# A scan layer and a convolution-attention layer: POOL's C product in two instructions, and inputs of the second layer put elsewhere

## The chip, the cores and the metric

The kernel runs on one core of a Trainium2 chip. A core has five engines that run side by side, each through its own instructions in order: PE (TensorE, matrix products), DVE (VectorE), ACT (ScalarE), POOL (GpSimd) and SP (SyncE, which here only issues transfers). ACT issues transfers too. Engines wait for each other at semaphores. The metric is the device time of the program in microseconds; of several runs the median is taken.

## The reference

Four images of 512 channels and 32 x 32 pixels go through two layers, each with a residual sum and a group normalisation in front. All is float32.

```python
x = x + L0(_gn(x), ...)
# L0, per image, L = 1024 tokens, 1024 inner channels, 16 states:
xn = layernorm(x over channels) * ln_w + ln_b
xm, z = split(xn @ W_in)
xs = silu(causal_depthwise_conv4(xm) + conv_b)
proj = xs @ W_x                      # 32 for dt, 16 for B, 16 for C
dt = softplus(proj[..., :32] @ W_dt + b_dt)
def step(h, inp):
    dt_t, B_t, C_t, x_t = inp
    h = exp(dt_t[..., None] * A) * h + (dt_t * x_t)[..., None] * B_t[:, None, :]
    return (h, einsum('bds,bs->bd', h, C_t))
y = scan(step) + xs * D
out = (y * silu(z)) @ W_out

x = x + L1(_gn(x), ...)
# L1, per image:
top, center = conv1x1(x, w_top), conv1x1(x, w_center)      # 64 channels each
bottom = conv3x3(x, w_bottom)
sp = softmax over all (n, m) of center^T top
x2 = x + (sp @ bottom) reshaped as it lies in memory
out = conv3x3(x2, w_out)
```

## The kernel before

**First layer.** The work is cut into units: image b, a pair of channel chunks e (2 x 128 channels), a half of the tokens h (512), and a state s: 4 x 4 x 2 x 16 = 512 units. A unit is written in `unit` (from line 814). ACT forms the decay exp(dt A) for each of the two chunks (L832). The input dt x B comes in one of two ways. For the nine states in `B_ON_ACT`, ACT scales rows (L844) and PE turns them into PSUM (L870). For the other seven, POOL multiplies (L859) with a broadcast row of B that SP fetches. DVE runs the recurrence as two scans, one for each chunk (L884), and in the first half copies the last column to a carry (L889). Then comes the product with C: for the four states in `C_ON_DVE` on DVE, per chunk (L900); for the other twelve on POOL, in one instruction over both chunks, 128 x 1024 elements (L906). PE adds the product of each chunk into its accumulator y (L913), turned back to tokens.

The order of the instructions is not that of the program text. Each piece of work is handed to `step` with its engine, a cost in us, what it reads and writes, and a priority; `Plan.issue` (from line 104) then plays the five engines forward with these costs and emits each instruction when its engine would take it. Buffers come in rings of a few slots: four for `h` (the tiles named da), four for `dbx`, five for `cbc` (broadcast rows of C). A slot is free again when its last user is done. The four `parts` and the tile `hc` tell the planner which chunk's scan a product needs: the product on POOL writes both parts, so it is placed after both scans, and both additions after it. Marked as filling, `transform` places on POOL the 18 pieces of weight transforms of the 3 x 3 convolutions; they go where there is room.

**Second layer.** The 3 x 3 convolutions are done with transformed tiles of the image and weights (6 row places in pairs (1, 2), (3, 4), (0, 5), 4 column places): `conv3` (L1439). Each of its 24 places is four accumulating matmuls of 128 x 512 (L1494), with a weight of 1 MB that SP loads into a ring of three (L1490). ACT and DVE evacuate the sums (L1502, L1510), and POOL adds them up (L1515, L1523, L1524, L1531). The inputs of a pair come from `first_inputs` (ACT L1393, POOL L1394, DVE L1396 and L1397) or `inputs`, then four DVE instructions in `spread` (L1374 to L1377).

For each pair of images a and a + 1 the order of the text is: conv3 b of image a, `attend(a)`, `scores(a + 1)`, conv3 b of a + 1, `attend(a + 1)`, conv3 o of a and `finish(a)`, conv3 o of a + 1 and `finish(a + 1)`, `scores(a + 2)`. In traces and text b0, o0, b1, o1 are these convolutions by image. `scores` makes eight tiles of scores, tag `st`, ring of eight: PE (L1324, then L1345), ACT copies them from PSUM (L1349), DVE takes maxima (L1350), ACT the exponentials (L1359). `attend` multiplies them with the convolution (L1546), in eight groups, and DVE adds each to the image (L1559). In the first two attentions it also does pieces of the output weights on DVE (L1421 to L1432). The PSUM ring `ps` of three serves scores, attention, statistics and `finish`; `pm` of five serves conv3.

`norm(b)` makes the next image: it takes the zero-bordered tile (`padded`, POOL memsets), loads the first layer's result in eight transfers on ACT's queue (L1285) into a tile with the tag `v`, which is that of the convolution's inputs (ring of two), and takes statistics on DVE (L1292, L1293). Two small PE products over the groups (L1299, L1303) and two ACT steps follow, then DVE normalises (L1306). Image 1's and image 3's norm runs beside the attention before; image 2's runs as `mid` inside conv3 o1. Images 0 and 2 share one buffer, 1 and 3 another.

In this layer the framework orders the instructions of an engine by its own estimate of readiness, within the dependencies. So a later function's instruction can stand ahead of an earlier one's on the same engine.

Of the kernel before, what the change touches and what calls it, by code (L numbers as in the profile page):

```python
# [8 lines left out]
F32 = mybir.dt.float32  # L9
# [6 lines left out]
P = 128  # L16
B, C, HH, WW = 4, 512, 32, 32
L = HH * WW
NCC = C // P
# [4 lines left out]
T = 512  # L24
# [145 lines left out]
def mamba_then_pab_kernel(  # L170
# [25 lines left out]
    nc = tc.nc  # L196
# [23 lines left out]
    brow = []  # L220
# [53 lines left out]
    with ExitStack() as l0:  # L274
# [539 lines left out]
        def unit(b, e, h, s, y):  # L814
# [86 lines left out]
                        [u, c_bc], [part], prio, holds=[hc],  # L901
                    )
            if not on_dve:
                step(
                    "POOL", 2.31,
                    lambda: nc.gpsimd.tensor_mul(hc(), hc(), c_bc().to_broadcast([P, 2, T])),  # L906
                    [c_bc], parts, prio, holds=[hc],
                )
            for j in range(2):

                def add(j=j):
# [348 lines left out]
    with ExitStack() as l1:  # L1260
# [15 lines left out]
        NMC = L // P  # L1276
        HR = T // WW

        def norm(b):

            xg = padded(b, *((cpool, "image"), (gp, "xg"))[b % 2])
            t = xp.tile([P, NCC, L], F32, tag="v", name=f"x1t_{b}")
            for c in range(NCC):
                for h in range(NH):
                    nc.scalar.dma_start(  # L1285
                        t[:, c, h * T : (h + 1) * T], x1[b][h][c * P : (c + 1) * P, :]
                    )
            mv = spool.tile([P, NCC, 2], F32, tag="mv", name=f"mv_l1_{b}")
            for c in range(NCC):
                bs = spool.tile([P, NH, 6], F32, tag="bs", name=f"bs_l1_{b}_{c}")  # L1290
                for h in range(NH):
                    nc.vector.bn_stats(bs[:, h, :], t[:, c, h * T : (h + 1) * T])  # L1292
                nc.vector.bn_aggr(mv[:, c, :], bs)  # L1293
            mean, rstd, dev = (
                spool.tile([P, NCC], F32, tag=n, name=f"{n}_l1_{b}")
                for n in ("gmean", "grstd", "gdev")
            )
            p1 = ps.tile([P, T], F32, tag="ps", name=f"pm_l1_{b}")
            nc.tensor.matmul(p1[:, :NCC], gm_sb, mv[:, :, 0], start=True, stop=True)  # L1299
            deviation(p1, mv, mean, dev)  # L1300
            yield
            p2 = ps.tile([P, T], F32, tag="ps", name=f"pv_l1_{b}")
            nc.tensor.matmul(p2[:, :NCC], gm_sb, dev, start=True, stop=True)  # L1303
            rsqrt(rstd, p2[:, :NCC])
            for c in range(NCC):
                nc.vector.tensor_scalar(  # L1306
                    xg[:, c, 1 : HH + 1, 1 : WW + 1],
                    t[:, c].rearrange("p (h w) -> p h w", w=WW),
                    mean[:, c : c + 1], rstd[:, c : c + 1], ALU.subtract, ALU.mult,
                )  # L1310
            image[b] = xg

        def scores(b, xg):

# [121 lines left out]
            for q in (1, 2):  # L1436
                nc.sync.dma_start(dst[q], o[:, q - 1])

        def conv3(name, xg, u, bias, first=None, late=None, mid=None):  # L1439

# [34 lines left out]
            y = [None] * 4  # L1475
            for pair in PAIRS:
                if pair == (1, 2):
                    v = first or first_inputs(name, xg)
                    if mid:
                        mid()  # L1480
                else:
                    v = spread(name, pair[0], inputs(pair))
                ns = []
                for k, p in enumerate(pair):
                    m = {}
                    for q in (2, 1, 0, 3):
                        if late and (p, q) == (5, 3):
                            late(y)
                        w = fp.tile([P, NCC, C], F32, tag="u", name=f"uw_{name}_{p}_{q}", bufs=3)
                        nc.sync.dma_start(w, u[q][p])  # L1490
                        m[q] = pm.tile([P, C], F32, tag="m", name=f"m_{name}_{p}_{q}")
                        extra = (p, q) == (1, 1)
                        for c in range(NCC):
                            nc.tensor.matmul(  # L1494
                                m[q], v[:, q, k, c, :], w[:, c, :],
                                start=(c == 0), stop=(c == NCC - 1 and not extra),
                            )
                        if extra:
                            nc.tensor.matmul(m[q], ones[0:1, :], bias, start=False, stop=True)
                    al = ALPHA[p]  # L1500
                    e = lp.tile([P, C], F32, tag="e2", name=f"e2_{name}_{p}", bufs=2)
                    nc.scalar.activation(e, m[2], AF.Copy, scale=al / 2)  # L1502
                    n = lp.tile([P, 2, C], F32, tag="n", name=f"n_{name}_{p}", bufs=2)
                    for o, src, w, add, op in (
                        (n[:, 0], m[1], al / 2, e, ALU.add),
                        (n[:, 1], m[1], al / 2, e, ALU.subtract),
                        (n[:, 0], m[0], al, n[:, 0], ALU.add),
                        (n[:, 1], m[3], -al, n[:, 1], ALU.add),
                    ):
# [25 lines left out]
            return y  # L1535

        def attend(b, xg, st, rp, xb, between, also):
# [4 lines left out]
            for k in range(NCC * NH):  # L1542
# [8 lines left out]
                if k == 0:  # L1551
# [4 lines left out]
                    for _ in between:  # L1556
                        pass
                img = xg[:, j, 1 + h * HR : 1 + (h + 1) * HR, 1 : WW + 1]
                nc.vector.scalar_tensor_tensor(  # L1559
                    img, pt.rearrange("p (h w) -> p h w", w=WW), rz, img,  # L1560
                    ALU.mult, ALU.add,
                )
                if also:
                    taps = piece_taps(also[k + 1]) if k + 1 < len(also) else None
                    piece(*ahead)
                    ahead = taps
                    if taps is None:
                        also = []

        dst = [out[b].rearrange("(c p) h w -> p c (h w)", p=P) for b in range(B)]  # L1570

# [41 lines left out]
                turn_back(b, j, o[j], y, 1)  # L1613
                (nc.scalar, nc.sync)[j % 2].dma_start(dst[b][:, j, :], o[j])

        def normed(b):
            for _ in norm(b):
                pass

        left = list(range(EARLY, NPC))  # L1620
        half = len(left) // 2
        st, rp = scores(0, image[0])
        for a in range(0, B, 2):
            for b in (a, a + 1):
                xb = conv3(f"b{b}", image[b], ub, brow[0])
                also = left[b * half : (b + 1) * half] if not a else []
                after, v = iter(()), None
                if b == a:
                    after = norm(b + 1)
                    next(after)  # L1630
                else:
                    v = first_inputs(f"o{a}", image[a])
                attend(b, image[b], st, rp, xb, after, also)
                if b == a:
                    st, rp = scores(b + 1, image[b + 1])
            finish(a, conv3(f"o{a}", image[a], uo, brow[1], v))
            if a + 2 == B:
                last(a + 1, image[a + 1], None)
                break
            y = conv3(f"o{a + 1}", image[a + 1], uo, brow[1], mid=lambda: normed(a + 2))  # L1640
            finish(a + 1, y)
            st, rp = scores(a + 2, image[a + 2])


# [55 lines left out]
```

## Time and profile before

| what | us |
|---|---|
| median of 3 runs | 3060.0 (3053.99 to 3060.22) |
| the profiled execution | 3048.93 |
| its span | 3047.1 |
| DVE busy in the span | 2402.3 |
| PE busy in the span | 2742.4 |
| POOL busy in the span | 2022.1 |
| ACT busy in the span | 1842.4 |

A profile line of a group gives source line, engine, operation, output and inputs by tile name, sizes and count, then after a bar the total busy us, the mean ns of one, and the engine's idle time just before the group with what ended most of it. A timeline line gives start and length in us, engine, line, what was done and how often; in square brackets how long the engine stood idle before and who released it. PE's records of a float32 product come in pairs: four matmuls show as x8. The share of a busy PE is not its share of peak.

### The profile page before, as it was taken

How to read it: one execution, taken by the hardware profiler on the slowest of the kernel's cores; microseconds unless marked ns; L12 is line 12 of the kernel's file. 1: busy time of each engine (PE TensorE's matmuls, PEld its weight loads, DVE VectorE, ACT ScalarE, POOL GpSimd, SP SyncE). 2: the span in 40 equal slices, each digit the busy share in tenths (PEclk: the TensorE clock that was granted, in tenths of full speed). 3: DMA queues.
4: the chain of work that ended last, by engine and by line, in shares of the span. 5: the costliest groups of instructions: out<-in, count | busy, mean ns of one | idle time of the engine just before them, and what ended most of it. 6: DMA issues, size and time to landing. Idle time of an engine off the chain costs nothing.

```text
span 3047.1 us, 35912 instructions
## 1 busy us (share of the span) xinstructions
PE 2742.4 (90%) x11512; PEld 1607.5 (53%) x11512; DVE 2402.3 (79%) x3171; ACT 1842.4 (60%) x3179; POOL 2022.1 (66%) x1047
## 2 busy tenths in 40 slices
PE   4789789999889999889999978799899999999998
PEld 2346556656666666556666655544344444444444
DVE  3469999989999989989999999976857575456164
ACT  4579989998789999789999888731110013030000
POOL 7899977899967889967889999843321331323132
PEclk8899999999999999989999999999999999999999
DMA  6766534567734567734566654748588896727497
GB/s 179 213 192 210 168 121 141 164 207 231 232 109 145 166 180 229 251 116 133 168 184 213 209 177 141 171 154 297 170 286 263 301 330 246 264 70 275 138 316 256
DMA packets 408947, 610.47 MB, mean 200 GB/s; under 512 B 46488, under 2 KB 245400, under 8 KB 384184
## 3 DMA queue, kind: packets, MB, share of 16 engines
q1 hardware_dynamic: 399952, 593.67, 61.8%
q10 hardware_dynamic: 8648, 14.26, 1.3%
q8 instruction: 92, 1.51, 0.2%
q14 instruction: 95, 0.78, 0.1%
q0 software_dynamic: 160, 0.26, 0.0%
HBM read 511.09 MB, written 96.99 MB: 200 GB/s over the span
## 4 chain that ended last, share of the span: by engine, by line
PE 45%; DVE 23%; ACT 16%; DMA 6%; issue 5%; POOL 4%; SPq 1%; ACTq 0%; DVEq 0%; POOLq 0%
PE m_o L1494 10%; PE m_b L1494 9%; DVE da L884 7%; PE y L913 5%; PE pz L394 4%; ACT sc L844 4%; PE pat L1546 4%; DVE u L884 3%; ACT da L832 3%; PE po L394 2%; PE u L870 2%; ACT u L832 2%; DVE dbx L884 2%; PE pxm L394 2%; PE psc L1345 2%
## 5 line engine op out<-in xcount | busy, mean ns | idle before, releaser
L906 POOL TENSOR_TENSOR da<-da,cbc 128x1024 f32<-128x1024 f32 x288 | 680.3, 2367 | 151.3 <-DVE carry_sb L889 63.6
L859 POOL TENSOR_TENSOR dbx<-dtx,bbc 128x1024 f32<-128x1024 f32 x224 | 529.6, 2368 | 59.1 <-PE y L913 34.9
L844 ACT ACTIVATE sc<-dtxt,bt_sb 128x256 f32<-128x256 f32 x1152 | 504.6, 497 | 46.2 <-PE u L870 46.0
L832 ACT ACTIVATE da<-dt,a_sb 128x512 f32<-128x512 f32 x576 | 395.0, 713 | 39.2 <-PE y L913 33.5
L884 DVE TENSOR_TENSOR_SCAN da<-da,carry_sb,u 128x512 f32<-128x512 f32 x288 | 356.0, 1262 | 27.3 <-PE u L870 22.0
L913 PE MATMUL y<-ident,da 128*128 128x128 f32 x2304 | 320.4, 283 | 58.3 <-POOL da L906 54.4
L870 PE MATMUL u<-ident,sc 128*128 128x128 f32 x2304 | 336.1, 278 | 35.3 <-DVE da L884 24.9
L913 PEld LDWEIGHTS y<-ident,da 128*128 128x128 f32 x2304 | 268.5, 145 | 161.2 <-POOL da L906 109.9
L884 DVE TENSOR_TENSOR_SCAN da<-da,u 128x512 f32<-128x512 f32 x288 | 348.8, 1211 | 3.9 <-PE u L870 3.6
L1494 PE MATMUL m_o<-uw_o,v_o 128*128 128x512 f32 x768 | 337.9, 599 | 4.4 <-DMA uw_o<-u_o 4.4
L1494 PE MATMUL m_b<-uw_b,v_b 128*128 128x512 f32 x768 | 333.4, 593 | 4.1 <-DMA uw_b<-u_b 4.1
L870 PEld LDWEIGHTS u<-ident,sc 128*128 128x128 f32 x2304 | 268.4, 143 | 112.2 <-DVE da L884 37.2
L832 ACT ACTIVATE u<-dt,a_sb 128x512 f32<-128x512 f32 x448 | 297.4, 681 | 36.8 <-DVE dbx L900 14.0
L394 PE MATMUL pxm<-xt,winc 128*128 128x345 f32 (+3 forms) x704 | 251.3, 499 | 29.3 <-DMA winc<-in_w_in_dram 16.5
L913 PE MATMUL y<-ident,dbx 128*128 128x128 f32 x1792 | 252.9, 279 | 23.7 <-POOL dbx L906 14.4
L913 PEld LDWEIGHTS y<-ident,dbx 128*128 128x128 f32 x1792 | 207.5, 143 | 99.7 <-issue 32.2
L394 PE MATMUL pz<-xt,winc 128*128 128x512 f32 x512 | 242.1, 600 | 11.7 <-ACT sz L707 2.1
L1494 PEld LDWEIGHTS m_o<-uw_o,v_o 128*128 128x128 f32 x768 | 145.9, 192 | 188.0 <-issue 180.7
L1494 PEld LDWEIGHTS m_b<-uw_b,v_b 128*128 128x128 f32 x768 | 145.0, 190 | 188.9 <-issue 179.5
L906 POOL TENSOR_TENSOR dbx<-dbx,cbc 128x1024 f32<-128x1024 f32 x96 | 226.7, 2362 | 26.0 <-DVE carry_sb L889 17.5
L1546 PE MATMUL pat<-y_b,st 128*128 128x512 f32 x512 | 221.6, 593 | 1.6 <-DVE rz L1555 1.5
L394 PEld LDWEIGHTS pxm<-xt,winc 128*128 128x128 f32 x704 | 132.0, 198 | 117.1 <-issue 62.1
(235 smaller groups left out, 4331.5 us busy)
## 6 DMA issues: line engine op xcount, KB each, us to landing
cbc<-bcd SPq DMA_DIRECT2D x512, 256.0 KB, 3.6
uw_b<-u_b SPq DMA_DIRECT2D x96, 1024.0 KB, 4.8
uw_o<-u_o SPq DMA_DIRECT2D x96, 1024.0 KB, 4.8
bbc<-bcd SPq DMA_DIRECT2D x224, 256.0 KB, 3.6
u_b<-work SPq DMA_DIRECT2D x192, 128.0 KB, 2.8
winc<-in_w_in_dram SPq DMA_DIRECT2D x72, 256.0 KB, 3.8
szd<-sz SPq DMA_DIRECT2D x32, 512.0 KB, 3.5
szl<-szd SPq DMA_DIRECT2D x32, 512.0 KB, 5.0
```

The costliest lines, as they stand in the source:

```text
L394: lambda k=k, lhs=lhs, rhs=rhs: nc.tensor.matmul(p()[:, at : at + cols], lhs(), rhs(), start=(k == 0), stop=(k == n - 1)),
L832: nc.scalar.activation(t, dt()[:, j], AF.Exp, scale=a_sb[:, at : at + 1])
L844: nc.scalar.activation(sc()[:, k], dtxt()[:, k], AF.Copy, scale=bt[:, at, s : s + 1])
L859: lambda: nc.gpsimd.tensor_mul(hc(), dtx(), b_bc().to_broadcast([P, 2, T])),
L870: nc.tensor.transpose(u()[:, k * P : (k + 1) * P], sc()[:, k, j, :], ident)
L884: nc.vector.tensor_tensor_scan(ht, *((hc()[:, j], u()) if on_act else (u(), hc()[:, j])), carry_sb[:, j, s : s + 1] if h else 0.0, ALU.mul ...
L906: lambda: nc.gpsimd.tensor_mul(hc(), hc(), c_bc().to_broadcast([P, 2, T])),
L913: nc.tensor.matmul(y[j]()[:, k, :], hc()[:, j, k * P : (k + 1) * P], ident, start=(s == 0 and k == 0), stop=(s == NS - 1 and k == NK - 1), ...
L1345: nc.tensor.matmul(pt, top[:, m * P : (m + 1) * P], center[:, h * T : (h + 1) * T], start=True, stop=True,)
L1494: nc.tensor.matmul(m[q], v[:, q, k, c, :], w[:, c, :], start=(c == 0), stop=(c == NCC - 1 and not extra),)
L1546: nc.tensor.matmul(pt, st[m][:, 2 * P * j + h : 2 * P * (j + 1) : 2], xb[m // 2][:, m % 2, :], start=(m == 0), stop=(m == NMC - 1),)
```

## The change

Three edits. The product with C on POOL is handed to the planner as two steps, one per chunk, of 128 x 512 elements each with a cost of 1.25 in place of one of 2.31. Each needs only its own chunk's scan, and each addition on PE only its own product. As the planner works from costs, the order of the first layer's instructions changes with it.

In the second layer `attend` returns its last sum, and `conv3` of the following image traces `first_inputs` under `issue_after` of it: the DVE instructions of the first pair's inputs may not stand ahead of that sum on DVE.

`norm` yields twice, after the statistics and after the first PE product, and takes the bordered tile only at its end. For image 2 it is called with `spare`: its four input tiles have the tag `st`, so they take slots of the scores, its loads and statistics stand in the text ahead of conv3 o0, its first product behind that convolution, and its rest behind `finish(0)`. The argument `mid` of conv3 is gone.

```diff
             if not on_dve:
-                step(
-                    "POOL", 2.31,
-                    lambda: nc.gpsimd.tensor_mul(hc(), hc(), c_bc().to_broadcast([P, 2, T])),
-                    [c_bc], parts, prio, holds=[hc],
-                )
+                for j in range(2):
+                    step(
+                        "POOL", 1.25,
+                        lambda j=j: nc.gpsimd.tensor_mul(hc()[:, j], hc()[:, j], c_bc()[:, 0]),
+                        [c_bc], [parts[j]], prio, holds=[hc],
+                    )
...
-        def norm(b):
-
-            xg = padded(b, *((cpool, "image"), (gp, "xg"))[b % 2])
-            t = xp.tile([P, NCC, L], F32, tag="v", name=f"x1t_{b}")
-            for c in range(NCC):
+        def norm(b, spare=False):
+
+            if spare:
+                ts = [xp.tile([P, L], F32, tag="st", name=f"x1t_{b}_{c}", bufs=NMC) for c in range(NCC)]
+            else:
+                t = xp.tile([P, NCC, L], F32, tag="v", name=f"x1t_{b}")
+                ts = [t[:, c] for c in range(NCC)]
+            for c, t in enumerate(ts):
...
+            yield
             p1 = ps.tile([P, T], F32, tag="ps", name=f"pm_l1_{b}")
...
-            for c in range(NCC):
+            xg = image[b] = padded(b, *((cpool, "image"), (gp, "xg"))[b % 2])
+            for c, t in enumerate(ts):
                 nc.vector.tensor_scalar(
...
                 if pair == (1, 2):
-                    v = first or first_inputs(name, xg)
-                    if mid:
-                        mid()
+                    with tc.issue_after(behind.ins) if behind else ExitStack():
+                        v = first or first_inputs(name, xg)
...
-                nc.vector.scalar_tensor_tensor(
+                ins = nc.vector.scalar_tensor_tensor(
                     img, pt.rearrange("p (h w) -> p h w", w=WW), rz, img,
...
+            return ins
...
         for a in range(0, B, 2):
+            ins = None
             for b in (a, a + 1):
-                xb = conv3(f"b{b}", image[b], ub, brow[0])
+                xb = conv3(f"b{b}", image[b], ub, brow[0], behind=ins)
...
                     after = norm(b + 1)
                     next(after)
+                    next(after)
...
-                attend(b, image[b], st, rp, xb, after, also)
+                ins = attend(b, image[b], st, rp, xb, after, also)
...
-            finish(a, conv3(f"o{a}", image[a], uo, brow[1], v))
+            if a + 2 < B:
+                after = norm(a + 2, True)
+                next(after)
+            y = conv3(f"o{a}", image[a], uo, brow[1], v)
+            next(after, None)
+            finish(a, y)
...
-            y = conv3(f"o{a + 1}", image[a + 1], uo, brow[1], mid=lambda: normed(a + 2))
-            finish(a + 1, y)
+            next(after, None)
+            finish(a + 1, conv3(f"o{a + 1}", image[a + 1], uo, brow[1]))
             st, rp = scores(a + 2, image[a + 2])
```

More of the change, by code (lines that the diff above doesn't have):

```diff
@@ L1277, in mamba_then_pab_kernel @@
         HR = T // WW
-        def norm(b):
-            xg = padded(b, *((cpool, "image"), (gp, "xg"))[b % 2])
-            t = xp.tile([P, NCC, L], F32, tag="v", name=f"x1t_{b}")
-            for c in range(NCC):
+        def norm(b, spare=False):
[5 more added lines that the diff above has]
+            for c, t in enumerate(ts):
                 for h in range(NH):
                     nc.scalar.dma_start(
-                        t[:, c, h * T : (h + 1) * T], x1[b][h][c * P : (c + 1) * P, :]
+                        t[:, h * T : (h + 1) * T], x1[b][h][c * P : (c + 1) * P, :]
                     )
             mv = spool.tile([P, NCC, 2], F32, tag="mv", name=f"mv_l1_{b}")
-            for c in range(NCC):
+            for c, t in enumerate(ts):
                 bs = spool.tile([P, NH, 6], F32, tag="bs", name=f"bs_l1_{b}_{c}")
                 for h in range(NH):
-                    nc.vector.bn_stats(bs[:, h, :], t[:, c, h * T : (h + 1) * T])
+                    nc.vector.bn_stats(bs[:, h, :], t[:, h * T : (h + 1) * T])
                 nc.vector.bn_aggr(mv[:, c, :], bs)
@@ L1304, in norm @@
             rsqrt(rstd, p2[:, :NCC])
-            for c in range(NCC):
+            xg = image[b] = padded(b, *((cpool, "image"), (gp, "xg"))[b % 2])
+            for c, t in enumerate(ts):
                 nc.vector.tensor_scalar(
                     xg[:, c, 1 : HH + 1, 1 : WW + 1],
-                    t[:, c].rearrange("p (h w) -> p h w", w=WW),
+                    t.rearrange("p (h w) -> p h w", w=WW),
                     mean[:, c : c + 1], rstd[:, c : c + 1], ALU.subtract, ALU.mult,
                 )
-            image[b] = xg
         def scores(b, xg):
@@ L1437, in piece, with conv3 @@
                 nc.sync.dma_start(dst[q], o[:, q - 1])
-        def conv3(name, xg, u, bias, first=None, late=None, mid=None):
+        def conv3(name, xg, u, bias, first=None, late=None, behind=None):
             def rows(a):
@@ L1614, in last @@
                 (nc.scalar, nc.sync)[j % 2].dma_start(dst[b][:, j, :], o[j])
-        def normed(b):
-            for _ in norm(b):
-                pass
         left = list(range(EARLY, NPC))
```

## The prediction

> **What bounds the kernel now.** I read the busy shares first, then the same in stretches, then the waits of POOL and PE, then PE's timeline through the second layer. The kernel has two halves with different limits: the first layer runs to about 2005 us of the 3047.1 us span, the second from there to the end. This is the window view of three stretches of the scans; the columns are length, then busy us and count of PE, PEld, DVE, ACT, POOL, the granted clock, DMA share and GB/s:
>
> ```profile
> 850.00:1100.00 250.00, 226.45 (x1181) 153.02 (x1179) 231.06 (x321) 229.67 (x379) 190.27 (x93) 0.97 0.46 142
> 1100.00:1300.00 200.00, 183.96 (x1015) 126.12 (x1015) 187.42 (x255) 173.89 (x315) 189.39 (x92) 0.97 0.74 233
> 1600.00:1950.00 350.00, 302.65 (x1785) 213.20 (x1786) 341.15 (x450) 300.63 (x550) 324.23 (x151) 0.99 0.62 182
> ```
>
> In the scans DVE is the fullest engine (97% in 1600 to 1950), POOL is close behind there (93%; 95% in 1100 to 1300) and has slack elsewhere (76% in 850 to 1100). Nothing in this layer is far from full. The groups of instructions price POOL's product, whole and half size:
>
> ```profile
> L906 POOL TENSOR_TENSOR da<-da,cbc 128x1024 f32<-128x1024 f32 x288 | 680.3, 2367 | 151.3 <-DVE carry_sb L889 63.6 <-DVE da L884 54.2 <-issue 15.7
> L906 POOL TENSOR_TENSOR dbx<-dbx,cbc 128x1024 f32<-128x1024 f32 x96 | 226.7, 2362 | 26.0 <-DVE carry_sb L889 17.5 <-DVE dbx L884 6.4 <-POOL da L906 1.1
> L793 POOL TENSOR_TENSOR dtx<-dt,xs 128x512 f32<-128x512 f32 x64 | 80.2, 1276 | 1.6 <-ACT dt L785 1.6
> ```
>
> The last column is POOL's idle time in front of the group: it waits on the second scan, or on the carry copy behind it. The waits of 400 to 1990 us (total, times, longest) show who suffers:
>
> ```profile
> POOL da L906 <- DVE carry_sb L889: 57.8, 29, 6.3
> POOL da L906 <- DVE da L884: 53.7, 32, 3.4
> ...
> PE y L913 <- POOL da L906: 45.0, 51, 2.8
> ```
>
> In the second layer PE is the bound (98% of 2600 to 3000), so each gap of PE is lost time. PE's timeline where image 1 follows the attention of image 0 (start, us, what, idle before and releaser):
>
> ```profile
> 2170.91 3.61 PE L1324 MATMUL pt<-xg,wt_sb 128*128 128x512 f32 x8
> 2176.76 3.71 PE L1324 MATMUL pt<-xg,wt_sb 128*128 128x512 f32 x8 [2.24 <-DVE xg L1559]
> 2180.31 1.88 PE L1494 MATMUL m_b<-uw_b,v_b 128*128 128x512 f32 x4
> 2188.05 5.36 PE L1345 MATMUL psc<-center,top 128*128 128x512 f32 x6 [5.86 <-DVE xg L1559]
> 2198.03 14.08 PE L1345 MATMUL psc<-center,top 128*128 128x512 f32 x26 [4.62 <-ACT st L1349]
> 2211.95 5.31 PE L1494 MATMUL m_b<-uw_b,v_b 128*128 128x512 f32 x12
> ```
>
> and the same matmuls one pair of images later, where they run without a stop:
>
> ```profile
> 2702.11 7.06 PE L1324 MATMUL pt<-xg,wt_sb 128*128 128x512 f32 x16
> 2709.00 1.88 PE L1494 MATMUL m_b<-uw_b,v_b 128*128 128x512 f32 x4
> 2710.72 13.90 PE L1345 MATMUL psc<-center,top 128*128 128x512 f32 x32
> 2724.45 5.31 PE L1494 MATMUL m_b<-uw_b,v_b 128*128 128x512 f32 x12
> ```
>
> The other two gaps that the change touches, at the start of the convolutions of images 0 and 1:
>
> ```profile
> 2353.83 8.70 PE L1494 MATMUL m_o<-uw_o,v_o 128*128 128x512 f32 x16 [3.05 <-DMA uw_o<-u_o]
> ...
> 2460.72 0.56 PE L1299 MATMUL pm_l<-mv_l,gm_sb 128*128 128x4 f32 x2 [6.05 <-DVE mv_l L1293]
> ```
>
> **What the Trainium skill says.** "GPSIMD Engine Reference", section 3.1, gives a two-input product about 2.6 cycles an element plus a software dispatch for each instruction. The trace agrees: (2367 - 1276) / 512 is 2.13 ns an element, which leaves 185 ns for each instruction, so two halves cost 185 ns more than one whole. "SBUF — State Buffer", section "SBUF: two separate sides", says that a DVE instruction with two SBUF inputs and a POOL instruction that reads SBUF exclude each other for a whole instruction. The trace agrees in the second layer: v_o at L1375 takes 3.37 us at 2386.16, beside POOL's L1523, and 1.22 us elsewhere. "DMA: Bandwidth & Descriptors", section "Issuing engines are not separate DMA queues", says that transfers from ACT and SP share the same engines; so loads moved onto ACT's queue take from SP's weights. At 2352 to 2356 us the windows show a DMA share of 0.94 to 1.04, which leaves nothing over.
>
> **Part 1, inputs behind the attention's last sum.** The five row and column instructions of image 1's first pair stood on DVE between the last two sums of image 0's attention (L1559), two of them at 3.55 us because of the exclusion. So the last sum ran at 2187.16 although its matmuls ended at 2170.9, and kept a PSUM buffer that the scores needed; after that ACT sat 13.94 us in e_o (L1393), ahead of the score copies, until DVE's rr_b. In the order of the changed program both sums come first and e_o stands behind the score copies. PE took 2211.95 - 2170.91 = 41.04 us; the twin at 2702.11 took 2724.45 - 2702.11 = 22.34. The difference is 18.7 us. I take 1.2 off, one v product, since m_b (q=2) now needs two row sums and one product after the sum: 17.5 us. Bounds: 14 if POOL's l_b blocks that product for its 3.5 us, 18.7. Cover elsewhere: image 3 gets the same order, and there the product must come within 2709.0 - 2703.0 = 6 us of the last sum; it needs 2 x 1.28 + 1.22 = 3.8, so nothing, at worst 2 us. The maxima (8 x 1.22) now mix with the second pair's products on DVE; that pair is due after 27 us of matmuls, so it costs nothing.
>
> **Part 2, image 2 in score tiles.** Its 8 loads (256 KB each), 8 statistics (0.68 us) and 4 merges move from the start of o1 to the start of o0. The 6.05 us go: PE's pm_l then has its inputs 90 us early. What is late next there is the last sum of `finish` (L1591), waiting on an output tile, but behind it stand only the evacuations, and five PSUM buffers give 17 us of cover. The price is at 2347 to 2371 us. ACT's eight issues stand before its e_o and e2; DVE's statistics stand before the last attention sum and before the first evacuation (L1510). In the program's waits the fourth to eighth load wait in part on o0's own weight loads (the sixth on the fourth weight, the eighth on the fifth, issued at 2359.13 and 2362.56), so the eighth lands near 2371 and the evacuation follows at about 2373 instead of 2363.7; the fifth PSUM buffer is full at 2353.83 + 5 x 3.44 + 1.12 = 2372.2 (3.44 us a weight, 1.12 the bias). That just fits. Three early loads, 0.77 MB at the 419 GB/s of those slices, may push the first weights by up to 1.8 us. I take 2 us for both, with bounds of 0 and 8 (2 MB at 300 GB/s plus 1 for PSUM). Net gain 4 us. The borders of the image (four memsets, 0.2 to 0.4 us) move to an idle POOL.
>
> **Part 3, the product in halves.** 384 units (288 + 96) x 185 ns add 71 us to POOL. Against that, a unit whose product waited for its second scan ends 2367 - 1276 = 1.09 us sooner, and its first half reaches PE sooner still. Adding up the chain of waits up to 2005 us, piece by piece, I find L906 on it 28 times with 50 us; so at best 28 x 1.09 = 30 us fall away, and as paths within tenths of a us lie beside it (DVE's whole idle time is 94 us of 400 to 1990) I count a third, 10 us. Against: in 600 to 850, 1100 to 1300 and 1600 to 1950 POOL gets 55, 45 and 85 x 0.185 = 10, 8 and 16 us more, which takes it to 99%, 99% and 97%. POOL then has no slack for jitter; I take 1% of these 800 us, 8 us. The planner also reorders: units shift by up to three places on POOL, 43 of 384 pairs get other work between their halves, and ACT gets 6 more table loads (1.28 us each, 8 us on an engine at 88%); 2 us. Sum: 0. Bounds: 25 us gained, 43 lost (the added share of 4.4% over some 1000 us if POOL set the pace in all of them).
>
> **Sum.** 17.5 + 4 + 0 = 21.5 us. The profiled execution took 3048.93 us, its span 3047.1; the median of the runs is 3060.0, 11 us above it. So a span of about 3025.6, and against the median 3060.0 - 21.5 = 3038.5, said as 3038.
>
> **The rivals.** First, the halves pay as well: POOL's and PE's waits above are 157 us, and if the chain gives its 30 us and the order is kind, 40 us are gained in all: 3020. Against it stands DVE at 97%. Second, the second layer gives its gain back at o0's start: the loads take 8 us and the product of part 1 the 3.5, so 14 - 2 = 12 us remain, and a bad order in the scans brings it to 3050. Third, slower: in the pure scan stretches POOL becomes the bound. Per sixteen units POOL has 12 C products, about 7 B products and one dtx pair: 12 x 2.55 + 7 x 2.37 + 2.55 = 49.7 us, and DVE now does sixteen in about 50 (85 C products, so 113 units, in 350 us). Once dbx and C products queue on POOL without gaps, each unit pays its 185 ns, and DVE waits on the four h buffers. It decides from a POOL share over 98%; it costs 28 to 43 us, less 21.5: 3066 to 3082, middle 3073. That POOL still waits 16 us on scans in 1600 to 1950 speaks against.
>
> **How the numbers follow.** Forecast 0.50, its own range 3028 to 3050; halves pay 0.17; gain given back 0.13; POOL bound 0.20. For 8 in 10 I take 3014 to 3068. A difference of 0.2% is 6 us, about what a measurement of this kernel tells from none. Faster: nearly all of the first (0.46), all of the second and half the third: 0.69. Slower: the fourth and a little of the first: 0.20. Within 0.2%: 0.11.
>
> **What would show it.** Right: PE takes about 23 us from the first pt to the second m_b of image 1; pm_l of image 2 has no wait; the gap before o0's first m_o is 3 to 6 us; the first layer ends near 2005 us; L906's idle time on DVE falls by half while its busy time is 980 us. Wrong: POOL at 99% through 1600 to 1950 with a later start of the scores, or DVE's evacuation holding PE at about 2372.

## The result and the profile after

| | before | after |
|---|---|---|
| median of 6 runs each, us | 3052.56 (3049.57 to 3060.22) | 3039.18 (3033.02 to 3046.45) |
| profiled execution, us | 3048.93 | 3037.96 |
| its span, us | 3047.1 | 3036.1 |
| first `psc` (start of the second layer's scores), us | 2014.4 | 2025.0 |
| from there to the end, us | 1032.7 | 1011.1 |
| POOL busy, us | 2022.1 | 2080.4 |

The ratio is 0.9957, interval 0.9937 to 0.9977: 13 us faster by the medians (7 to 19), where 21.5 were forecast. The table's rows on `psc` split the two profiled executions: the second layer became 21.6 us shorter, the first layer 10.6 us longer.

PE's timeline of the changed kernel, where image 1 follows the attention of image 0 (start, us, what, idle before and releaser):

```profile
2183.34 7.05 PE L1329 MATMUL pt<-xg,wt_sb 128*128 128x512 f32 x16
2190.24 1.90 PE L1498 MATMUL m_b<-uw_b,v_b 128*128 128x512 f32 x4
2191.97 13.90 PE L1350 MATMUL psc<-center,top 128*128 128x512 f32 x32
2205.70 5.31 PE L1498 MATMUL m_b<-uw_b,v_b 128*128 128x512 f32 x12
...
2237.93 2.41 PE L1498 MATMUL m_b<-uw_b,v_b 128*128 128x512 f32 x5 [1.64 <-ACT e_b L1506]
```

From the first pt to the second m_b it is 2205.70 - 2183.34 = 22.36 us, and no bracket stands in the first four lines: the three gaps are gone. In the last line the evacuation on ACT is late by 1.64 us; before, PE did not wait for it there. Image 3 has the same line with 1.43 us. The same view at the start of image 0's second convolution and at image 2's statistics:

```profile
2349.39 8.68 PE L1498 MATMUL m_o<-uw_o,v_o 128*128 128x512 f32 x16 [4.52 <-DMA uw_o<-u_o]
...
2434.68 0.28 PE L1304 MATMUL pm_l<-mv_l,gm_sb 128*128 128x4 f32 x2
```

The wait of 6.05 us at pm_l is gone, and the wait for the weights grew from 3.05 to 4.52.

The gaps are not the whole gain. Of the 41.04 us before, the three gaps are 2.24 + 5.86 + 4.62 = 12.72; another 6 us are matmuls that ran more slowly. Behind the two longer gaps the 32 records of psc took 5.36 + 14.08 us, where they take 13.90 without a gap. It is the same behind the gap at pm_l, six records before and six in the changed kernel:

```profile
2461.14 5.35 PE L1494 MATMUL m_o<-uw_o,v_o 128*128 128x512 f32 x6
```

```profile
2443.34 2.82 PE L1498 MATMUL m_o<-uw_o,v_o 128*128 128x512 f32 x6
```

From start to start, such records are 0.85 us apart for a few us and then 0.43. The granted clock of PE between 2190 and 2216 us was 0.81 in the kernel before and 1.00 in the changed one. Over the second layer PE is busy 995.3 us before and 988.3 after with the same 2388 instructions: 7 of the 21.6 us are faster matmuls, and the rest is idle time.

In the scans, the window view of the same three stretches as before (length, then busy us and count of PE, PEld, DVE, ACT, POOL, clock, DMA share, GB/s):

```profile
850.00:1100.00 250.00, 228.59 (x1173) 151.18 (x1171) 230.64 (x322) 233.00 (x384) 195.90 (x136) 0.98 0.44 139
1100.00:1300.00 200.00, 186.10 (x1030) 127.15 (x1028) 183.82 (x242) 171.58 (x313) 196.64 (x138) 0.98 0.73 228
1600.00:1950.00 350.00, 309.79 (x1782) 216.19 (x1780) 339.77 (x453) 300.03 (x552) 338.76 (x234) 0.97 0.59 184
```

POOL rose from 95 to 98% in 1100 to 1300 and from 93 to 97% in 1600 to 1950, while DVE did no more work there than before. The product's groups (us busy, mean ns, then POOL's idle time in front of them and its releasers):

```profile
L907 POOL TENSOR_TENSOR da<-da,cbc 128x512 f32<-128x512 f32 x576 | 725.4, 1279 | 117.8 <-DVE carry_sb L889 50.9 <-DVE da L884 42.0 <-issue 18.9
L907 POOL TENSOR_TENSOR dbx<-dbx,cbc 128x512 f32<-128x512 f32 x192 | 242.3, 1278 | 25.7 <-DVE carry_sb L889 12.0 <-issue 5.9 <-DVE dbx L884 5.3
```

and the waits of PE and ACT in 400 to 1990 us (total us, times, longest), three lines of the kernel before and then the changed one:

```profile
ACT sc L844 <- PE u L870: 42.3, 41, 3.5
...
PE y L913 <- POOL dbx L906: 12.7, 15, 2.6
...
PE y L913 <- DVE dbx L900: 8.0, 13, 1.3
```

```profile
ACT sc L844 <- PE u L870: 71.4, 52, 5.3
...
PE y L914 <- POOL dbx L907: 22.8, 29, 2.8
PE y L914 <- DVE dbx L900: 20.1, 18, 2.5
PE y L914 <- POOL da L907: 17.4, 32, 2.1
```

PE waits less for the product (57.7 us for both kinds before, 40.2 now). But it waits 20.1 us for DVE's product, 8.0 before, and ACT waits 71.4 us for PE to turn the scaled input rows (u) back, 42.3 before. Such totals wander by several us between profiles of the same first layer: in the four of them below, ACT's wait is 41.6 to 48.1 us. One profile of each kernel can't say which of these cost the 10.6 us, nor whether the split did. So the first group of experiments takes the parts of the change apart.

### The profile page after: what moved, and what is told of

It reads as the page before. It is cut to its first block, busy times and chain, and to the rows that moved or that the text cites. A ratio compares the mean times of both kernels' runs of the same rounds, so it can differ in the third digit from the quotient of the medians.

```text
span 3036.1 us, 36289 instructions
## 1 busy us (share of the span) xinstructions
PE 2746.5 (90%) x11512; PEld 1608.2 (53%) x11512; DVE 2386.2 (79%) x3171; ACT 1849.4 (61%) x3185; POOL 2080.4 (69%) x1431
## 4 chain that ended last, share of the span: by engine, by line
PE 39%; DVE 28%; ACT 14%; POOL 8%; DMA 5%; issue 5%; SPq 0%; ACTq 0%; DVEq 0%; POOLq 0%
PE m_o L1498 10%; DVE da L884 9%; PE m_b L1498 8%; PE po L394 4%; DVE u L884 4%; PE pat L1550 4%; ACT sc L844 3%; PE y L914 3%; DVE dbx L884 3%; DVE dbx L900 2%; ACT da L832 2%; PE u L870 2%; POOL da L907 2%; ACT u L832 2%; POOL dbx L859 2%
## 5 line engine op out<-in xcount | busy, mean ns | idle before, releaser
L907 POOL TENSOR_TENSOR da<-da,cbc 128x512 f32<-128x512 f32 x576 | 725.4, 1279 | 117.8 <-DVE carry_sb L889 50.9
L870 PE MATMUL u<-ident,sc 128*128 128x128 f32 x2304 | 342.6, 281 | 28.1 <-DVE da L884 23.0
L914 PE MATMUL y<-ident,da 128*128 128x128 f32 x2304 | 339.6, 280 | 30.9 <-POOL da L907 27.7
L914 PE MATMUL y<-ident,dbx 128*128 128x128 f32 x1792 | 275.6, 284 | 58.0 <-DVE dbx L900 30.5
L907 POOL TENSOR_TENSOR dbx<-dbx,cbc 128x512 f32<-128x512 f32 x192 | 242.3, 1278 | 25.7 <-DVE carry_sb L889 12.0
L394 PE MATMUL pz<-xt,winc 128*128 128x512 f32 x512 | 244.7, 596 | 10.6 <-ACT sz L707 2.1
```

The source lines that it names most:

```text
L394: lambda k=k, lhs=lhs, rhs=rhs: nc.tensor.matmul(p()[:, at : at + cols], lhs(), rhs(), start=(k == 0), stop=(k == n - 1)),
L870: nc.tensor.transpose(u()[:, k * P : (k + 1) * P], sc()[:, k, j, :], ident)
L907: lambda j=j: nc.gpsimd.tensor_mul(hc()[:, j], hc()[:, j], c_bc()[:, 0]),
L914: nc.tensor.matmul(y[j]()[:, k, :], hc()[:, j, k * P : (k + 1) * P], ident, start=(s == 0 and k == 0), stop=(s == NS - 1 and k == NK - 1), ...
```

## The experiments

Two theories of the first layer's loss stand against each other: **load**, the time that the extra instructions take on POOL, and **order**, the planner's new sequence with finer and dearer steps. A third holds that the difference is the scatter of two profiles. Each kernel is compared with runs of the kernel before on the same chip. All results:

| kernel | ratio to before (interval) | us from the ratio |
|---|---|---|
| second layer's edits only | 0.9938 (0.9925 to 0.9951) | -19 |
| split only | 1.0031 (1.0019 to 1.0043) | +9.5 |
| halves, old order | 1.0019 (1.0010 to 1.0028) | +6 |
| whole product planned at 2.50 | 0.9985 (0.9978 to 0.9991) | -5 |
| split, halves planned at 1.155 | 1.0033 (1.0022 to 1.0044) | +10 |
| whole product plus one column | 1.0039 (1.0024 to 1.0053) | +12 |
| inputs behind the last sum only | 0.9948 (0.9934 to 0.9961) | -16 |
| image 2 in score tiles only | 0.9992 (0.9985 to 0.9999) | -2.4 |
| second layer's edits, product at 2.50 | 0.9934 (0.9919 to 0.9949) | -20 |
| second layer's edits, product at 2.40 | 0.9931 (0.9914 to 0.9948) | -21 |
| columns where POOL has slack | 1.0025 (1.0014 to 1.0036) | +7.6 |
| columns where POOL is nearly full | 1.0048 (1.0036 to 1.0060) | +14.7 |

**The second layer's edits alone.** The changed kernel, with the product whole again:

```diff
-                for j in range(2):
-                    step("POOL", 1.25,
-                        lambda j=j: nc.gpsimd.tensor_mul(hc()[:, j], hc()[:, j], c_bc()[:, 0]),
-                        [c_bc], [parts[j]], prio, holds=[hc])
+                step("POOL", 2.31,
+                    lambda: nc.gpsimd.tensor_mul(hc(), hc(), c_bc().to_broadcast([P, 2, T])),
+                    [c_bc], parts, prio, holds=[hc])
```

> The changed kernel with the C product whole again: only the two edits of the second layer remain. Theory L (the split itself costs the first layer its 10.6 us, by POOL's load or by the order it gives, and the second layer's edits bring 21.6): first layer ends within 2 us of before's 2014.4, second layer takes 1011 us, total about 3031 (3049 - 21 + what noise adds, ratio near 0.993 to before), some 8 to 10 us faster than the whole change. Theory N (the first layer's time wanders between builds and runs, the split has no part in it): first layer ends again near 2025 and the total is near 3039. Theory H (the halves pay in the first layer and something else of the change costs it): slower than the whole change, above 3045.

Measured: 3033.95 us. The profiled first layer reached psc at 2019.5, within neither the 2 us of one theory nor the 2025 of the other; the second layer took 1012.8, as expected. The scatter is real: of the four profiled kernels whose first layer is the same program (before, this one, and the two below with one second-layer edit each) psc starts at 2014.4, 2019.5, 2014.0 and 2023.0. So of the 10.6 us between the first two profiles several can be chance, and the runs have to decide. The scatter of the runs goes with the clock that PE was granted: of 30 runs of the kernel before on one chip, the fastest (3043.92 us) had a mean of 0.974 and the slowest (3061.89) of 0.966. The medians of the six kernels below that add only instructions on POOL are 0.967 to 0.970, those of the kernel before 0.969 to 0.971 on the four chips. Which of the two drives the other was not tried, so a part of their loss may come by PE's clock.

**The split alone.** The kernel before with the split of the product only (the first piece of the diff, part 3 of the prediction).

> The kernel before with the split of the C product alone. Theory L: first layer ends near 2025, total about 3058 to 3060 (+9 to +11, ratio 1.003), and POOL's share in 600 to 850 us rises to 97% as in the whole change. Theory N: within 3 us of before. Theory H: 8 to 10 us faster than before.

Measured: +9.5 us, 5.8 to 13.1. psc starts at 2025.9. The split makes the kernel slower, and all profiles taken together place the loss in the first layer: in the seven kernels with a plain whole product psc starts at 2014.0 to 2023.0, in the seven with extra POOL instructions (halves, or the columns below) at 2025.0 to 2032.5. The scatter is not the cause. How much of the 9.5 us falls there is less sure: in this profile the second layer took 1037.3 us, 4.6 more than before with the same instructions in the same order. In the other seven kernels without the second layer's edits it took 1026.7 to 1033.8, and in the four with both edits 1011.1 to 1013.2. With the second layer's -19 it gives about -9, and the whole change measured -13, within the two intervals.

**Halves in the old order.** One planner step of the old cost issues both halves:

```diff
-                step("POOL", 2.31,
-                    lambda: nc.gpsimd.tensor_mul(hc(), hc(), c_bc().to_broadcast([P, 2, T])),
-                    [c_bc], parts, prio, holds=[hc])
+                def both():
+                    for j in range(2):
+                        nc.gpsimd.tensor_mul(hc()[:, j], hc()[:, j], c_bc()[:, 0])
+                step("POOL", 2.31, both, [c_bc], parts, prio, holds=[hc])
```

> The kernel before, in which each C product is issued as two half instructions back to back, at the place and cost that the planner gave the whole one: POOL has the 384 extra instructions and PE may start on the first half, but PE, DVE, ACT and SP keep before's order exactly. Theory L1 (load: 384 x 185 ns more on POOL delays the B products and everything behind them): POOL busy near 968 us in L907-like rows, first layer 8 to 11 us longer, total +8 to +11 (about 3058). Theory L2 (order: the split made the planner re-time its steps, and that new order is what costs): no loss here, and the earlier first half may give up to 10 us: total between -10 and +1.

Measured: +6 us, 3 to 8.5, with before's order on every engine. So by the points the larger part of the loss is not the planner's. The profiles show no part of the planner's at all: psc starts at 2027.9 here and at 2025.0 to 2027.4 in the three kernels with the split, but this profiled execution was 5 us above its kernel's median, so this says little. In this kernel the waits of 400 to 1990 us read:

```profile
POOL da L906 <- DVE carry_sb L889: 33.1, 26, 3.9
POOL da L906 <- DVE da L884: 30.3, 37, 2.7
...
PE y L913 <- POOL da L906: 24.3, 43, 2.2
...
PE y L913 <- DVE dbx L900: 7.1, 12, 1.1
PE y L913 <- POOL dbx L906: 5.7, 12, 0.8
```

PE's waiting for the product fell from 57.7 to 30.0 us, and POOL's for the second scan and its carry copy (da alone) from 111.5 to 63.4. The halves do what they are for, and the kernel is still slower.

**A dearer plan, the same work.** The whole product, planned at 2.50 us:

```diff
-                    "POOL", 2.31,
+                    "POOL", 2.50,
```

> The kernel before with the C product as one instruction, but planned at 2.50 us (the sum of the two halves' planned costs) instead of 2.31: no work is added, only the planner's order moves. Theory L1 (load): within 3 us of before. Theory L2 (the order that a dearer product gives): +5 to +11 us in the first layer.

Measured: -5 us, 2.7 to 6.7. Neither theory said so. The profile does not place the gain in the first layer, whose order is what changed: psc starts at 2016.7, 2.3 us later than before, and it is the second layer, with the same instructions in the same order, that took 1026.7 us instead of 1032.7. The three kernels planned at 2.40 or 2.50 start psc at 2016.7 to 2019.1, inside the range of the four planned at 2.31. So the runs are 5 us apart, and that the new order gave it is not shown.

**The halves planned at 1.155.** The split alone, with one number changed:

```diff
-                        "POOL", 1.25,
+                        "POOL", 1.155,
```

> The kernel before with the split, each half planned at 1.155 us, so that the two add up to the 2.31 of the whole product (the change plans 1.25 each). POOL does the same work as in the split alone; only the planner's order differs. Load theory (the 71 us that the halves add to POOL cost about 6 us, as halves in the old order did, and the rest of the split's 9.9 is an order that happens to be worse): +4 to +8 against before. If the finer steps are what costs, whatever they are planned at: +9 to +11, like the split alone. If the finer steps give an order that pays once the cost is right: below +3.

Measured: +10 us, 6.7 to 13.4, like the split planned at 1.25. The waits of the split at 1.25 alone, and then of this kernel:

```profile
ACT sc L844 <- PE u L870: 73.9, 54, 5.3
...
PE y L914 <- DVE dbx L900: 21.4, 20, 2.5
PE y L914 <- POOL dbx L907: 19.9, 24, 2.8
PE y L914 <- POOL da L907: 17.8, 32, 2.1
```

```profile
ACT sc L844 <- PE u L870: 81.6, 60, 5.3
...
PE y L914 <- POOL da L907: 43.5, 64, 2.4
PE y L914 <- POOL dbx L907: 30.2, 28, 2.9
...
PE y L914 <- DVE dbx L900: 6.7, 8, 1.6
```

The plan's cost moves PE's wait from POOL to DVE and back, but ACT's wait for PE is long in both (47.4 us with the halves in the old order). By the points, what the planner makes of two separate steps costs some 4 us more than the old order with the same halves; the intervals overlap and psc starts no later, so these 4 us are not shown.

**The load without the earlier start.** Behind each whole product POOL multiplies one column that nobody reads; no part of the result is touched.

```diff
+        scrap = cpool.tile([P, 1], F32, tag="scrap", name="scrap")
...
+                def both():
+                    nc.gpsimd.tensor_mul(hc(), hc(), c_bc().to_broadcast([P, 2, T]))
+                    nc.gpsimd.tensor_mul(scrap, dp_sb[:, 0:1], dp_sb[:, 0:1])
+                step("POOL", 2.31, both, [c_bc], parts, prio, holds=[hc])
```

> The kernel before; behind each whole C product POOL multiplies one column (128x1) into a scrap tile that nobody reads. The extra column adds an instruction without a finer wait: priced by the rows of before at 185 + 2 = 187 ns, so 384 x 187 = 72 us more POOL, the same load as the halves, while PE still waits for the whole product. All engines keep before's order. Theory A (halves in the old order cost +6.0 because a load of about +16 is partly repaid by 10 from PE's earlier start): about +14 to +18 here. Theory B (the earlier start is worth nothing and the load is all): +5 to +7. Theory C (it is not the load but the halves' narrower operand that costs): 0 to +2.

Measured: +12 us, 7 to 16; the point is below A's 14 to 18 and above B's 5 to 7, and theory C's 0 to 2 is ruled out. The group of the columns, two waits, and a few steps of POOL's timeline:

```profile
L907 POOL TENSOR_TENSOR scrap<-dp_sb 128x1 f32<-128x1 f32 x384 | 77.2, 201 | 0.0
```

```profile
PE y L914 <- POOL da L906: 59.7, 76, 3.0
...
PE y L914 <- POOL dbx L906: 15.5, 17, 2.7
```

```profile
675.65 2.36 POOL L906 TENSOR_TENSOR da<-da,cbc 128x1024 f32<-128x1024 f32 x1
677.95 0.21 POOL L907 TENSOR_TENSOR scrap<-dp_sb 128x1 f32<-128x1 f32 x1
678.10 2.38 POOL L906 TENSOR_TENSOR dbx<-dbx,cbc 128x1024 f32<-128x1024 f32 x1
```

The group says 201 ns for a column, but the next product starts 678.10 - 677.95 = 0.15 us after the column does: records of neighbours overlap. Over all instructions that the next one follows without a gap, the median from start to start is 2.320 us for a whole product (before), 1.233 for a half (after) and 0.145 for a column. Two halves thus add 2 x 1.233 - 2.320 = 0.146 us, 384 of them 56 us, and the columns 56: equal loads. POOL's busy time confirms it: 2077.2 with the halves in the old order and 2077.9 here, against 2022.1. With equal load and order, PE's wait for the product is 75.2 us here and 30.0 with the halves. So the load costs about 12 us (7 to 16), which is shown. That the earlier start gives about 6 back is the difference of two points whose intervals overlap: the shorter waits speak for it, and it is not shown.

**Where the load costs.** Columns only in the channel groups whose scans run where POOL had slack (two to a product), or only in the others (one to a product):

```diff
+                    nc.gpsimd.tensor_mul(hc(), hc(), c_bc().to_broadcast([P, 2, T]))
+                    for k in range(2 * (b * NDC + 2 * e + h in (4, 5, 6, 11, 12, 13, 14, 19, 20, 21, 22, 23))):
+                        nc.gpsimd.tensor_mul(scrap, dp_sb[:, 0:1], dp_sb[:, 0:1])
```

and in the other kernel

```diff
+                    nc.gpsimd.tensor_mul(hc(), hc(), c_bc().to_broadcast([P, 2, T]))
+                    if b * NDC + 2 * e + h not in (4, 5, 6, 11, 12, 13, 14, 19, 20, 21, 22, 23):
+                        nc.gpsimd.tensor_mul(scrap, dp_sb[:, 0:1], dp_sb[:, 0:1])
```

> The kernel before; two one-column multiplies behind each whole C product, but only in the twelve channel groups whose scans run where POOL was 74 to 79% busy (400 to 600, about 810 to 1070 and 1290 to 1600 us): 288 x 201 ns = 58 us more POOL, all of it in slack. Saturation theory (POOL's extra load costs only where POOL is nearly full): within 3 us of before. Latency theory (each extra instruction delays the next product by 0.2 us, wherever it stands): in proportion to the load, 12.0 x 58 / 77 = +9.

> The kernel before; one such multiply behind each C product of the other twenty channel groups, whose scans run where POOL was 93 to 97% busy: 240 x 201 ns = 48 us more POOL, all of it where POOL is nearly full. Saturation theory: nearly the whole of the 12.0 us that all 384 cost, +9 to +12. Latency theory: 12.0 x 48 / 77 = +7.5, and less than the kernel with 58 us in the slack.

Measured: +7.6 (4.3 to 11) in the slack, +14.7 (11 to 18) where POOL is nearly full. POOL's busy time rose by 2073.5 - 2022.1 = 51.4 and 2056.9 - 2022.1 = 34.8 us. The columns of the two kernels, slack first, then full:

```profile
L908 POOL TENSOR_TENSOR scrap<-dp_sb 128x1 f32<-128x1 f32 x288 | 56.5, 196 | 11.3
```

```profile
L908 POOL TENSOR_TENSOR scrap<-dp_sb 128x1 f32<-128x1 f32 x240 | 47.5, 198 | 0.0
```

A us of load costs 7.6 / 51.4 = 0.15 us in the slack and 14.7 / 34.8 = 0.42 where POOL is nearly full. So saturation is not the whole of it: a product that comes later costs even where POOL has a quarter of its time free. It weighs more than twice as much where POOL has almost none; neither theory said both. The slack kernel has two columns to a product and the one with all columns has one, so its half, 3.8 us, goes with the 14.7: 18.5 us (13 to 24) against the measured 12 (7 to 16). The intervals overlap, so whether the parts simply add is open, and a rate from here is not to be used to better than a factor of two.

**The second layer's edits one by one.** The kernel before with `behind` alone (the inputs of images 1 and 3 behind the last sum), then with the score tiles for image 2 alone (no `behind`):

```diff
-                    v = first or first_inputs(name, xg)
+                    with tc.issue_after(behind.ins) if behind else ExitStack():
+                        v = first or first_inputs(name, xg)
...
-                xb = conv3(f"b{b}", image[b], ub, brow[0])
+                xb = conv3(f"b{b}", image[b], ub, brow[0], behind=ins)
...
```

> The kernel before with one edit of the second layer alone: the first inputs of images 1 and 3 issued behind the last sum of the attention before. By the trace of the whole change this removes 18.7 us of gaps between the first pt and the second m_b of image 1, and gives about 1.3 + 1.4 back in new waits for e_b: 16 us faster, total near 3036, ratio 0.9945 to 0.9955. The rival, that part of the 18.7 is only there if image 2 has left the v buffer as well: 8 to 12 us faster.

> The kernel before with the other edit of the second layer alone: image 2 normed from score tiles, around image 0's second convolution. By the trace of the whole change pm_l's 6.05 us wait goes and 1.5 to 2.5 us come back as weight waits at the start of that convolution: 3.5 to 4.5 us faster, ratio 0.9985 to 0.999. If the waits only move (weights late by as much as was saved): within 1 us of before.

Measured: -16 us (-20 to -12) and -2.4 (-4.6 to -0.3). PE's timeline of the first at image 1:

```profile
2172.77 7.06 PE L1324 MATMUL pt<-xg,wt_sb 128*128 128x512 f32 x16
2180.52 1.96 PE L1495 MATMUL m_b<-uw_b,v_b 128*128 128x512 f32 x4 [0.69 <-DVE v_b L1374]
2182.31 13.90 PE L1345 MATMUL psc<-center,top 128*128 128x512 f32 x32
2196.04 5.31 PE L1495 MATMUL m_b<-uw_b,v_b 128*128 128x512 f32 x12
```

It needs no help from image 2's buffers: 23.27 us, 17.8 below before's 41.04. In all five kernels with this edit the stretch takes 22.3 to 23.4 us, in the nine without it 40.9 to 41.7. The second kernel, at image 0's second convolution:

```profile
2363.52 9.90 PE L1497 MATMUL m_o<-uw_o,v_o 128*128 128x512 f32 x16 [5.06 <-DMA uw_o<-u_o]
...
2450.04 0.28 PE L1303 MATMUL pm_l<-mv_l,gm_sb 128*128 128x4 f32 x2
```

pm_l's wait is gone and 2.0 us of it come back as a wait for the weights (5.06 against 3.05). This wait is 4.5 to 6.0 us in all five kernels with this edit and 2.2 to 3.4 in the nine without. The forecast put it down to the earlier loads on the same DMA engines; that cause was not tried by itself. In this profile the second layer is 6.9 us shorter than before (1025.8 against 1032.7) and the first layer, with the same instructions, 8.6 us longer; so the 2.4 us of the runs may hold more than the edit.

**Two orders for the second layer's edits.** The whole product again, planned at 2.50 and at 2.40 instead of 2.31:

> The second layer's edits with the C product whole and planned at 2.50 us. If the two gains are in different layers and simply add (18.5 from the second layer's edits, 4.8 from the order at 2.50): ratio 0.9920 to 0.9930, some 23 us below before and about 10 below the whole change. If the order's 4.8 was noise between programs: ratio 0.9938, like the second layer's edits alone.

> The same with the product planned at 2.40 us, close to the measured 2.367. If the gain at 2.50 comes from a plan nearer to what POOL takes: as at 2.50 or better, ratio 0.9915 to 0.993. If it is one order's luck among many: anywhere between 0.992 and 0.997, with no trend over 2.31, 2.40, 2.50.

Measured: -20 and -21 us, against -19 with 2.31. The 5 us by which the plan at 2.50 beat the kernel before don't show here; the intervals (0.9919 to 0.9949, 0.9914 to 0.9948) hold both that gain and none. All three versions with a whole product have points 6 to 8 us below the changed kernel's; their intervals overlap with its own, so that they beat it rests on the split's separate loss of 9.5 us rather than on this comparison.

## Why the prediction was right, and where not

- **Direction and size.** Faster by about 13 us instead of 21.5. The second layer gave about what was said, 21.6 in the trace and 19 (15 to 23) in the runs, against 21.5. Most of the shortfall is in part 3. That the measured 3039 lies 1 us from the forecast 3038 is luck: the gain was put 8 us too high, and the median it was taken from, 3060.0 of three runs, was 7 us above the 3052.56 of six.
- **Part 1, 17.5 us: right.** Alone 16 us (12 to 20). The comparison with the twin took in the slower matmuls behind the gaps, about 6 of the 18.7 us, which the prediction did not tell apart from the gaps. The 1.2 us for one v product was 0.69 us of waiting when tried alone and nothing in the whole change, and the waits for e_b (1.64 and 1.43 us) were not foreseen as such; that image 3 could lose up to 2 us was.
- **Part 2, 4 us: inside the interval.** Alone 2.4 us (0.3 to 4.6) in the runs. The 6.05 us went, and with them some 2.5 us of slow matmuls behind pm_l (5.35 against 2.82) that the prediction did not count. The price of 2 us at the start of o0 was 2.0 when tried alone and 1.5 in the whole change, within the 3 to 6 us gap that was said; two weight waits of 0.48 and 0.52 us follow in the whole change. PE was not held at 2372: the fit of the five PSUM buffers was right. The Trainium skill, "DMA: Bandwidth & Descriptors", section "Issuing engines are not separate DMA queues", says that transfers share the same engines whichever engine issues them, and it agrees with these waits: the loads stand on ACT's queue and the weights on SP's, and the weights became late.
- **Part 3, sum 0: the step that was mis-sized.** It measured +9.5 us, inside its bounds of -25 to +43. Its terms: (a) the load on POOL, 71 us, was 56, as the 185 ns for each instruction came from durations whose records overlap; from start to start it is 146. (b) What the load costs, put at 8 us from saturation alone, measured about 12 (7 to 16): load also costs in the slack, 0.15 us for each us. (c) The earlier start, put at 10, gave about 6 by the points, though PE's waits for the product halved in the old order. (d) The reorder, put at 2, is about 4 by the points. Terms (c) and (d) are differences of points whose intervals overlap, so only (a) and the size of (b) are measured.
- **The rival "POOL becomes the bound" did not come.** In the three stretches POOL reached 97, 98 and 97% where 99, 99 and 97 were said, and DVE stayed at 97% in 1600 to 1950. But its mechanism, each unit paying for its extra instruction, is at work in part: the load costs in the slack too, so a point below which it costs nothing (98%) was the wrong picture.
- **What would show it.** The first layer was said to end near 2005, where it had ended; by psc it ended 10.6 us later. L906's idle time on DVE, said to fall by half, fell from 135 to 104 us in 400 to 1990 us in the changed kernel (80 with the halves in the old order), while its busy time is 968 us, where 980 were said.

## What to carry to other kernels

A finer split buys shorter waits with added load, and on an engine that is 93 to 97% busy the load can win even when the waits it aims at fall by half; price the extra instruction from start to start of neighbours, not from the durations. Try each part of a change alone when a planner orders the work: here the gain and the loss lay in different layers. A wait of the engine that sets the pace can cost more than its length: here the matmuls behind it ran at half their pace. Before a 10 us difference between two profiles is explained, look at how far two profiles of the same instructions lie apart.

## What the runs showed of the hardware

- The durations of neighbouring POOL instructions overlap in the records: a 128x1024 product lasts 2367 ns and the next instruction starts 2320 ns after its start; a 128x1 product lasts 201 ns and the next starts after 145.
- The extra instruction costs POOL the same 145 to 146 ns whether it is a 128x1 product or the second half of a product.
- One and the same first layer reached the second at 2014.0 to 2023.0 us in four profiled kernels. Differences of 3 to 6 us are there by 600 us, and some of them vanish again.
- Behind each of the 32 waits of PE above 4 us in the second layers of the 14 profiles, the next matmul records of 128x512 start 0.85 us apart, for some 3 to 7 us, before they return to 0.43. Shorter waits show it in some places and not in others.
